# Cross-attention and a quantised feed-forward on one core: all transpositions moved from DMA to TensorE

## The chip, the cores and the metric

The kernel runs on one core of a Trainium2 chip. The core has five engines with instruction streams of their own: TensorE (PE; its weight loads are shown apart as PEld), VectorE (DVE), ScalarE (ACT), GpSimd (POOL) and SyncE (SP), which issues this kernel's DMAs. Each engine takes its work in program order and waits on semaphores for what others make. The metric is the device time of one execution in microseconds (us), lower is better; the time before is 1144.62 us, the median of 3 runs.

## The reference

One block of a transformer on x of shape (8, 1024, 512) with a context of shape (8, 64, 384):

```python
x = x + xattn(layernorm(x), ctx)     # 8 heads of 64, softmax over 64 context rows, then @ Wo + bo
x = x + ffn(layernorm(x))

def ffn(x):                          # inner width 2048
    gate = silu(bitlinear(x, w_gate))
    up = bitlinear(x, w_up)
    return bitlinear(gate * up, w_down)

def bitlinear(x, w):
    s = 127 / max|x| per row         # activations rounded to whole numbers of -128..127
    t = 1 / mean|w|                  # weights rounded to -1, 0, 1
    return (clip(round(x * s)) / s) @ (clip(round(w * t)) / t).T
```

All inputs and outputs are fp32.

## The kernel before

The 8192 rows of x are cut into 64 tiles of 128 rows (`NU` = 64); 8 tiles belong to one batch. The kernel is a single Python function that writes out every engine's order by hand (`manual_schedule`), so the order of the calls is the order on each engine.

**Attention.** For each batch the query and key weights are folded into one matrix `score_w` (`score_products`), and the value and output weights into `value_w` (`value_products`). A tile's scores are x transposed times `score_w`; its attention output is the transposed probabilities times `value_w`. Both are fp32. From tile 8 on, two tiles form a `Pair`, whose product is made of seven quarter products instead of eight (`Seven`); GpSimd forms the sums of blocks that this needs (`add`, and `weight_sums` for the weights). Tiles 0 to 7 are computed alone.

**Feed-forward.** x is normalised, rounded by a magic constant (`round_x` on ScalarE, `shrink_x` on GpSimd) to whole numbers in bf16 (`xq`), and transposed to `xq_t`. `gate_up(s)` makes 512 columns of gate and of up, 8 matmuls with fp8 weights, four times. `gated` applies silu and multiplies. `quantise_h` rounds the product in two halves (ScalarE L614, GpSimd L615) to `hq`, which is transposed to `hq_t`; `output` multiplies it by the down weights in 16 matmuls (L621).

**The pipeline.** A head (the long string `order`) loads the inputs, prepares the first score and value weights, rounds the three feed-forward matrices to -1, 0, 1 in 24 halves, and computes tiles 0 to 6 as far as it can. Each half goes through `round_half`, `shrink_half`, on some paths `clip_half`, and `turn_half`, which transposes it into its place. The loop then runs k from 0 to 64. Iteration k holds the gate and up products of tile k, the rounding of tile k-1's intermediate, the down product of tile k-1, the rounding of x of tile k+1, and attention work for tiles up to k+8: in even iterations a pair's seven score products, in odd ones a pair's seven output products, set between the four calls of `gate_up`. In some batches' iterations the next score and value weights are made too. The last iterations (58 to 63) are arranged apart: rounding comes after the second `gate_up`, and the down products of tiles 61 and 62 stand in iteration 63, after the last tile's rounding (`quantise_h_last`).

**Transpositions.** TensorE needs the left operand transposed. In the head, x of tiles 0 to 7 and the probabilities of tiles 0 to 5 are transposed on TensorE into PSUM (`transpose_x` L353, `transpose_p` L412) and copied out by ScalarE (L357, L416). Everything else is transposed by DMA, issued by SyncE:

- fp32 x and probabilities: GpSimd splits the fp32 words into two 16-bit halves (`split`, L329), one DMA transposes both (L331), and `join` (L338, on ScalarE or GpSimd) puts the words together again;
- `xq` (`turn_x`, L560) and `hq` (L616, and L652 for the last tile), which are bf16;
- the weight halves (`turn_half`, L763), whose fp8 pairs are moved as 16-bit words; this is why the fp8 operands are read with every other byte in the matmuls, and why `as_chunks` and `in_chunks` write even and odd columns apart.

**PSUM.** There are 8 banks. `next_bank` hands them out in turn: banks 0 to 5 for general use, 6 and 7 for projections and products in the head, and in the loop 6 for a pair's running sum "x" and 7 for "y" and "z".

Of the kernel before, what the change touches and what calls it, by code (L numbers as in the profile page):

```python
# [29 lines left out]
def xattn_ffn_kernel(  # L30
# [37 lines left out]


    rounds = {"product": [6, 7], "bank": [0, 1, 2, 3, 4, 5], "x": [6], "z": [7], "y": [7]}  # L70

# [15 lines left out]
    ident = const.tile([P, P], F32, name="ident")  # L87
    make_identity(nc, ident)
    magic = const.tile([P, 1], F32, name="magic")
    nc.vector.memset(magic, MAGIC)  # L90
# [233 lines left out]

    def split(src, name, room):
        halves = apool.tile([P, 2, D], U16, tag=f"{room}2", name=f"split_{name}")
        nc.gpsimd.tensor_copy(halves, src.bitcast(U16).rearrange("p (d h) -> p h d", h=2))  # L329
        halves_t = apool.tile([P, 2 * ND, P], U16, tag=f"{room}2_t", name=f"split_t_{name}")  # L330
        nc.sync.dma_start_transpose(out=halves_t, in_=halves.rearrange("p h d -> p (h d)"))  # L331
        return halves_t

    def join(copy, halves_t, name):
        whole = apool.tile(
            [P, ND, P], F32, tag=f"{name[0]}_t", name=f"{name[0]}_t_{name}", bufs=2
        )
        copy(  # L338
            whole.rearrange("p c t -> p (c t)").bitcast(U16).rearrange("p (m h) -> p h m", h=2),
            halves_t.rearrange("p (h c) t -> p h (c t)", h=2),  # L340
        )
        return whole


    class Attention:
# [13 lines left out]
        def split_x(self):  # L359
            self.x = x_tile(self.i)  # L360
            self.x2_t = split(self.x, f"x_{self.name}", "x")

        def join_x(self):
            self.x_t = join(nc.scalar.copy, self.x2_t, f"x_{self.name}")

        def split_p(self, room="p"):
            self.p2_t = split(self.p.rearrange("p h l -> p (h l)"), f"p_{self.name}", room)

        def join_p(self, copy):
            self.p_t = join(copy, self.p2_t, f"p_{self.name}")  # L370

# [69 lines left out]

    def weight_sums(w, sums):

        w11, w12, w21, w22 = (block(w, i, j) for i in range(2) for j in range(2))
        nc.gpsimd.tensor_tensor(sums[0], w12, w11, ALU.subtract)
        nc.gpsimd.tensor_tensor(w12, w22, w12, ALU.subtract)
        nc.gpsimd.tensor_tensor(sums[1], w22, sums[0], ALU.subtract)
        nc.gpsimd.tensor_tensor(sums[2], w21, sums[1], ALU.subtract)

# [74 lines left out]
    class FeedForward:  # L524
# [30 lines left out]
        def turn_x(self):  # L555
            if self.i >= LATE:
                self.xq_t = late_xq_t[:, ts(self.i % 8, ND), :]
            else:
                self.xq_t = fpool.tile([P, ND, P], BF16, tag="xq_t", name=f"xq_t_{self.name}")
            nc.sync.dma_start_transpose(out=self.xq_t, in_=self.xq)  # L560

# [49 lines left out]
        def quantise_h(self, i):  # L611
            self.hq_t = hq_t_rooms[self.i % 2]
            h, hq = self.h[i], hq_rooms[i]
            nc.scalar.activation(h, h, AF.Identity, bias=magic, scale=self.scale)  # L614
            nc.gpsimd.tensor_scalar(as_chunks(hq), in_chunks(h), -MAGIC, 1.0, ALU.add, ALU.mult)  # L615
            nc.sync.dma_start_transpose(out=self.hq_t[:, ts(i, NF // 2), :], in_=hq)  # L616

# [17 lines left out]
        def quantise_h_last(self):  # L635
# [15 lines left out]
            for i in (1, 0):  # L651
                nc.sync.dma_start_transpose(  # L652
                    out=self.hq_t[:, ts(i, NF // 2), :], in_=hq_rooms[i]
                )
# [59 lines left out]
    def spread_total(i):  # L714
        held["mean", i] = pm = product(f"wtot_ps_{i}")
        nc.tensor.matmul(pm[:, 0:1], lhsT=ones, rhs=held["total", i], start=True, stop=True)
# [24 lines left out]
    def shrink_half(n):  # L741
        tag = ("x2", "p2", "x2_t", "p2_t")[n % 4]
        held["half", n] = wq = apool.tile([P, 2 * D], BF16, tag=tag, name=f"wq_{n}")
        if rounded_by[n] == "a":
            nc.gpsimd.tensor_scalar(wq, part(n), -MAGIC, 1.0, ALU.add, ALU.mult)
        else:
            held["half", n] = signs = wq[:, :D].bitcast(FP8)
            nc.scalar.activation(signs, part(n), AF.Sign, bias=minus_magic, saturate=False)

    def clip_half(n):  # L750
        wq = held["half", n]
        clipped = apool.tile([P, 2 * D], FP8, tag="clipped", name=f"clipped_{n}", bufs=2)
        held["half", n] = clipped
        nc.vector.tensor_scalar(clipped, wq, -1.0, 1.0, ALU.max, ALU.min, saturate=False)

    def turn_half(n):
        i, c, g = n // 8, n % 8 // 2, n % 2
        w_t = weights[i][1]
        if i < 2:
            to = w_t[:, 4 * c + 2 * g :][:, :2].rearrange("p n c f -> p (n c) f")  # L760
        else:
            to = w_t[:, ts(g, 4), ts(c, P)]
        nc.sync.dma_start_transpose(out=to, in_=held["half", n].bitcast(U16))  # L763

# [18 lines left out]
    def ffn_stats(part):  # L783
# [4 lines left out]
        elif part == "b":  # L788
            f.rs = inverse_std(f.mv[:, 1:2], f.name)
        elif part == "c":  # L790
            f.normalise()
            f.scale_x()
        else:
            {"d": f.round_x, "e": f.shrink_x, "f": f.turn_x}[part]()

    def keep(table, i, value):
# [55 lines left out]
        inverse_std.0 copy_v.1.a v.3 sum.0.a v_late.1 copy_v.3.v mean_var.1 copy_v.0.v  # L852
        inverse_std.1 score.3 sum.1.v score.1 score_copies.3.a score_copies.1.a
        score_copies.3.v sum.2.a score_copies.1.v copy_v_late.1.v score.0
        sum.3.a score.2 score_copies.0.v k_late.3 score_copies.2.v score_copies.2.a total.0
# [19 lines left out]
        load_x.3 round.20.g round.22.v turn.15 shrink.16 sums.4 round.18.g transpose_p.3  # L875
        turn.16 shrink.17 residual.2 scores.5 ffn.b copy_p.3 round.19.g turn.17 mean_var.6
        shrink.18 probabilities.4 ffn.c turn.18 shrink.19 attend.3 inverse_std.6 round.23.g
        shrink.20 turn.19 maximum.5 ffn.d turn.20 shrink.21 exp.5 transpose_p.4 residual.3
        ffn.e transpose_x.6 copy_p.4 clip.21 ffn.f copy_x.6 sums.5 attend.4 shrink.22 turn.21
        probabilities.5 shrink.23 turn.22 turn.23 residual.4  # L880
    """
    for entry in order.split():
        kind, n, *on = entry.split(".")
        kinds[kind](int(n) if n.isdigit() else n, *on)
    load_x(4)
    weight_sums(score_w[1], score_sums)


# [17 lines left out]
    pairs = [Pair(i) for i in range(NU // 2)]  # L906
    rounds["product"] = rounds["bank"]
    FIRST = NT // 2
    for k in range(NU + 1):
# [9 lines left out]
        soft = pairs[(k + LEAD - 1) // 2] if not even and FIRST <= (k + LEAD - 1) // 2 < NU // 2 else None  # L919
        joined = pairs[(k + LEAD - 2) // 2] if even and FIRST <= (k + LEAD - 2) // 2 < NU // 2 else None  # L920
        done = pairs[(k + 3) // 2] if not even and 3 <= k < NU - 6 else None
# [3 lines left out]
        if k == 0:  # L925
# [4 lines left out]
            norm_stats(att[LEAD + 1], quant, after)  # L930
        elif (k == 1 or even or k > NU - 6) and k != NU - 6 and quant:
            norm_stats(quant, extra, after)
# [9 lines left out]
        if not last and k != 2 and not (soft and k > NU - 10):  # L942
            round_next(1 if scored or soft else 2)
        if after and even:
            after.split_x()
# [18 lines left out]
        if k == 1:  # L964
            alone.scores(every)
            alone.less_maximum()
            quant.normalise()
# [10 lines left out]
        if soft:  # L978
            soft.tiles[0].sums()
            soft.tiles[0].probabilities()  # L980
            soft.tiles[0].split_p()
        if not even and 1 < k < NU - 6 and (quant or after):
            norm_stats(quant, extra, after)
        early = quant and not soft and k < NU - 6
        if f:
# [15 lines left out]
        if early and k < 2:  # L1001
            quant.quantise_x()
        if k == 1:
            weight_sums(value_w[0], value_sums)
        if soft:
# [27 lines left out]
        if f:  # L1033
            f.gate_up(2)
            f.intermediate(2)
        part("x4")()
        if after and even:
# [6 lines left out]
        if f:  # L1044
            f.gate_up(3)
            f.gated(3)
        if k in (0, 2):
            att[LEAD + k // 2].join_p(nc.gpsimd.tensor_copy)
        if joined and k < NU - 6:
            joined.tiles[1].join_p(nc.gpsimd.tensor_copy)  # L1050
        if quant and not early:
            quant.quantise_x()
        if soft:
            soft.tiles[0].join_p(nc.scalar.copy)
            soft.tiles[1].split_p("px"[k == NU - 7])
            if k == NU - 7:
                soft.tiles[1].join_p(nc.gpsimd.tensor_copy)

# [20 lines left out]
        if k == 1:  # L1079
            alone.sums()  # L1080
            alone.probabilities()
            alone.split_p()
        if after and even:
# [18 lines left out]
        for i in downs(k):  # L1102
            if i == NU - 1:
                ffn[i].output_last()
            else:
                ffn[i].output()


# [29 lines left out]
```

## Time and profile before

| what | value |
|---|---|
| median of 3 runs | 1144.62 us (1144.59 to 1144.74) |
| the profiled execution's own time | 1144.76 us |
| its span, from first to last instruction | 1142.9 us |
| mean granted TensorE clock | 1.000 |
| instructions | 16576 |
| DMA packets, bytes | 320358, 126.93 MB |
| packets under 512 B | 304784 |
| busy share of the 16 DMA engines by queue 1 | 50.8% |

The page gives each engine's busy time, then the chain of work that ended last, followed back from the last instruction. A line of a group reads: line of the source, engine, operation, what is written from what, shape, count, then busy time and mean duration. In a timeline each row is a start, a length, an engine and a line; several instructions in a row are merged and counted with "x". Matmuls overlap, so the distance from one start to the next says what one costs, and its duration doesn't. In a table by windows, each engine has its busy time and in brackets its number of instructions.

### The profile page before, as it was taken

The numbers are of one execution on the slowest core, as the hardware profiler recorded it, in microseconds if no ns is written. First come the engines' busy times: TensorE is split into PE (matmuls) and PEld (weight loads), VectorE is DVE, ScalarE is ACT, GpSimd is POOL, SyncE is SP. The second block draws the span as 40 slices with busy tenths as digits, with TensorE's granted clock in tenths as the row PEclk, the third lists the DMA queues.
The fourth block names the chain that finished last, engine by engine and source line by source line (L and its number), as shares of the span: only waits on it lengthen the run. The fifth ranks groups of instructions, "written<-read, shape, count | busy, mean of one in ns | idle before, by whom it ended". The sixth has DMA issues, their size and how long they took to land.

```text
span 1142.9 us, 16576 instructions
## 1 busy us (share of the span) xinstructions
PE 1132.5 (99%) x5332; PEld 673.7 (59%) x5332; DVE 965.6 (84%) x1908; ACT 725.6 (63%) x935; POOL 743.3 (65%) x850
## 2 busy tenths in 40 slices
PE   8999999999999999999999999999999999999998
PEld 7444566556656666556566666655655665565544
DVE  5887888888888888888898888888888888998885
ACT  3975765766665666666666665676765566666443
POOL 0566776576767757677676867657776676775422
PEclk9999999999999999999999999999999999999999
DMA  9874445455455555354454545545436544453344
GB/s 350 270 158 86 101 87 117 91 106 95 88 114 111 107 102 106 84 93 111 94 114 107 97 100 90 103 106 106 94 79 124 112 101 107 106 102 65 65 96 98
DMA packets 320358, 126.93 MB, mean 111 GB/s; under 512 B 304784, under 2 KB 305552, under 8 KB 319760
## 3 DMA queue, kind: packets, MB, share of 16 engines
q1 hardware_dynamic: 320272, 125.88, 50.8%
q8 instruction: 42, 0.69, 0.2%
q14 instruction: 44, 0.36, 0.1%
HBM read 34.08 MB, written 16.78 MB: 44 GB/s over the span
## 4 chain that ended last, share of the span: by engine, by line
PE 92%; DVE 3%; DMA 2%; POOL 1%; SPq 1%; issue 1%; ACT 0%; DVEq 0%; POOLq 0%; ACTq 0%
PE u_f L574 19%; PE g_f L574 18%; PE down_f L621 18%; PE x_o_pair L482 9%; PE x_s_pair L482 8%; PE z_o_pair L482 4%; PE z_s_pair L482 4%; PE y_o_pair L482 2%; PE y_s_pair L482 2%; PE scores_a L376 2%; PE attn_a L422 2%; DMA score_w<-in_L_ffn_w_gate_dram 2%; PE value_ps L267 1%; PE score_ps L249 1%; PE v_late L205 1%
## 5 line engine op out<-in xcount | busy, mean ns | idle before, releaser
L589 ACT ACTIVATE ln_room<-g_f,dq_x_f 128x512 f32<-128x512 f32 x216 | 148.1, 686 | 210.4 <-PE g_f L574 210.3
L574 PEld LDWEIGHTS <-xq_t_f 128*128 128x128 bf16 x1728 | 169.1, 98 | 186.4 <-issue 2.6
L621 PE MATMUL down_f<-arena,room 128*128 128x512 fp8e4 x1008 | 227.9, 379 | 0.0
L574 PE MATMUL u_f<-arena,xq_t_f 128*128 128x512 fp8e4 x864 | 221.7, 379 | 0.6 <-DVE x_room L428 0.6
L574 PE MATMUL g_f<-wg_t,xq_t_f 128*128 128x512 fp8e4 x864 | 221.7, 379 | 0.0
L615 POOL TENSOR_SCALAR room<-room 128x1024 bf16<-128x1024 f32 x126 | 142.5, 1134 | 104.3 <-ACT room L614 99.1
L590 DVE SCALAR_TENSOR_TENSOR room<-u_f,dq_x_f,ln_room 128x512 f32<-128x512 f32 x216 | 160.9, 745 | 32.0 <-POOL rs_f L298 21.7
L614 ACT ACTIVATE room<-room,magic,scale_h_f 128x1024 f32<-128x1024 f32 x126 | 155.4, 1240 | 22.8 <-DVE scale_h_f L318 22.3
L621 PEld LDWEIGHTS <-room 128*128 128x128 bf16 x1008 | 96.6, 98 | 123.8 <-issue 9.1
L602 DVE TENSOR_REDUCE am_h_f<-room 128x1 f32<-128x1024 f32 x126 | 153.1, 1215 | 2.3
L551 POOL TENSOR_SCALAR xq_f<-ln_room 128x512 bf16<-128x512 f32 x64 | 41.9, 655 | 149.6 <-ACT ln_room L547 146.9
L406 POOL TENSOR_TENSOR p_a<-p_a,rc_a 128x512 f32<-128x512 f32 x64 | 67.1, 1049 | 25.0 <-DVE rc_a L402 14.2
L625 DVE SCALAR_TENSOR_TENSOR x_room<-down_f,dq_h_f,x_room 128x512 f32<-128x512 f32 x63 | 47.1, 747 | 37.7 <-PE down_f L621 37.6
L338 ACT COPY x_t_x_a<-split_t_x_a 128x1024 uint16<-128x1024 uint16 x56 | 75.6, 1350 | 0.0
L391 DVE TENSOR_TENSOR p_a<-p_a,mx_a 128x512 f32<-128x512 f32 x56 | 62.6, 1117 | 1.9
L329 POOL COPY split_x_a<-x_room 128x1024 uint16<-128x1024 uint16 x56 | 63.6, 1137 | 0.0
L329 POOL COPY split_p_a<-p_a 128x1024 uint16<-128x1024 uint16 x58 | 60.1, 1036 | 2.0
L547 ACT ACTIVATE ln_room<-ln_room,magic,scale_x_f 128x512 f32<-128x512 f32 x64 | 51.4, 804 | 8.7 <-DVE scale_x_f L318 8.7
L521 DVE TENSOR_TENSOR x_room<-x_room,x_o_pair 128x256 f32<-128x256 f32 x116 | 48.3, 416 | 8.8 <-PE x_o_pair L482 6.7
L589 ACT ACTIVATE ln_room<-g_f,value_w 128x512 f32<-128x512 f32 x40 | 27.1, 684 | 42.5 <-PE g_f L574 39.4
L574 PEld LDWEIGHTS <-score_w 128*128 128x128 bf16 x320 | 31.3, 98 | 36.1
L286 DVE BATCH_NORM_STATS2 st_a<-x_room 128x6 f32<-128x512 f32 x64 | 42.5, 664 | 6.0 <-DMA x_room<-in_x_dram 6.0
(193 smaller groups left out, 2207.4 us busy)
## 6 DMA issues: line engine op xcount, KB each, us to landing
x_room<-in_x_dram SPq DMA_DIRECT2D x32, 512.0 KB, 4.1
out_dram<-x_room SPq DMA_DIRECT2D x31, 512.0 KB, 2.6
room<-in_L_ffn_w_gate_dram SPq DMA_DIRECT2D x3, 1024.0 KB, 14.4
room<-in_L_ffn_w_down_dram SPq DMA_DIRECT2D x2, 1024.0 KB, 6.3
room<-room SPq DMA_TRANSPOSE x126, 3.2
arena<-in_L_xattn_Wq_dram SPq DMA_DIRECT2D x1, 1024.0 KB, 7.3
score_w<-in_L_ffn_w_gate_dram SPq DMA_DIRECT2D x1, 1024.0 KB, 17.4
wo_sb<-in_L_xattn_Wo_dram SPq DMA_DIRECT2D x1, 1024.0 KB, 15.5
```

The source lines that it names most:

```text
L329: nc.gpsimd.tensor_copy(halves, src.bitcast(U16).rearrange("p (d h) -> p h d", h=2))
L338: copy(whole.rearrange("p c t -> p (c t)").bitcast(U16).rearrange("p (m h) -> p h m", h=2), halves_t.rearrange("p (h c) t -> p h (c t)", h=2),
L391: nc.vector.tensor_tensor(self.p, pm, mx.unsqueeze(2).to_broadcast([P, HEADS, L]), ALU.subtract)
L406: nc.gpsimd.tensor_tensor(self.p, self.p, rc, ALU.mult)
L482: nc.tensor.matmul(pm, lhsT=p[:, c, :], rhs=w[:, c, :], start=first and c == 0, stop=c == 1, skip_group_check=not first,)
L574: nc.tensor.matmul(ps, lhsT=self.xq_t[:, c, :], rhs=rhs.rearrange("p n (f e) -> p n e f", e=2)[:, :, c % 2], start=(c == 0), stop=(c == ND ...
L589: nc.scalar.activation(sg, pg, AF.Silu, scale=self.dq[:, 0:1])
L590: nc.vector.scalar_tensor_tensor(h[:, ts(s % 2, 512)], pu, self.dq[:, 1:2], sg, ALU.mult, ALU.mult)
L602: nc.vector.tensor_reduce(self.am[:, s // 2 : s // 2 + 1], h, AX.X, ALU.max, apply_absolute_value=True)
L614: nc.scalar.activation(h, h, AF.Identity, bias=magic, scale=self.scale)
L615: nc.gpsimd.tensor_scalar(as_chunks(hq), in_chunks(h), -MAGIC, 1.0, ALU.add, ALU.mult)
L621: nc.tensor.matmul(pm, lhsT=self.hq_t[:, f, :], rhs=every_other(wd_t[:, f // 2, :], f % 2), start=(f == 0), stop=(f == NF - 1),)
```

## The change

No DMA transposes any more. Every transposition is a TensorE instruction that writes into PSUM, followed by a copy to SBUF:

- x and probabilities of all tiles use the fp32 transposes of the head, four per tile, and a ScalarE copy; `split` and `join` go.
- `xq` and each half of `hq` go through the new `turn_chunks`: 4 or 8 bf16 transposes into one bank, then one copy (ScalarE for xq and the first half of hq, VectorE for the second half). The calls are put in a list and carried out by `turn_now` at three places of an iteration: after the third `gate_up`, after the fourth, and after the down products. The last tile's two halves are turned where they stand.
- the weight halves are kept in bf16 and transposed in 8 pieces into a bank of their own (bank 5 in the head); VectorE clips them to -1, 0, 1 on the way out of PSUM and writes fp8, even and odd columns in one instruction each.
- bank 5 joins the general banks when the head ends; the loop's products use the general banks from iteration 1 on. Some calls move: two entries of `order`, the four `weight_sums` of the first value weights, and the statistics of iteration 2.

```diff
-    rounds = {"product": [6, 7], "bank": [0, 1, 2, 3, 4, 5], "x": [6], "z": [7], "y": [7]}
+    rounds = {"product": [6, 7], "bank": [0, 1, 2, 3, 4], "weights": [5], "x": [6], "z": [7], "y": [7]}
...
-    def split(src, name, room):
...
-    def join(copy, halves_t, name):
...
+    def turn_chunks(to, chunks, name, copy):
+        n = len(chunks)
+        pt = bank(f"turn_tp_{name}").bitcast(BF16)[:, : n * P].rearrange("p (n m) -> p n m", n=n)
+        for c, chunk in enumerate(chunks):
+            nc.tensor.transpose(pt[:, c, :], chunk, ident_b)
+        copy(to, pt)
+
+    later = []
+
+    def turn_now():
+        for turn in later:
+            turn()
+        later.clear()
...
         def join_x(self):
-            self.x_t = join(nc.scalar.copy, self.x2_t, f"x_{self.name}")
+            self.transpose_x()
+            self.copy_x()
...
-        def join_p(self, copy):
-            self.p_t = join(copy, self.p2_t, f"p_{self.name}")
+        def join_p(self, copy=None):
+            self.transpose_p()
+            self.copy_p()
...
-    def weight_sums(w, sums):
+    def weight_sums(w, sums, which=(1, 3, 2, 4)):
...
-            nc.sync.dma_start_transpose(out=self.xq_t, in_=self.xq)
+            chunks = [self.xq[:, ts(c, P)] for c in range(ND)]
+            to = self.xq_t
+            later.append(lambda: turn_chunks(to, chunks, f"xq_{self.name}", nc.scalar.copy))
...
-            nc.sync.dma_start_transpose(out=self.hq_t[:, ts(i, NF // 2), :], in_=hq)
+            chunks = [hq[:, ts(f, P)] for f in range(NF // 2)]
+            to, copy = self.hq_t[:, ts(i, NF // 2), :], (nc.scalar.copy, nc.vector.tensor_copy)[i]
+            later.append(lambda: turn_chunks(to, chunks, f"hq_{self.name}_{i}", copy))
...
             for i in (1, 0):
-                nc.sync.dma_start_transpose(
-                    out=self.hq_t[:, ts(i, NF // 2), :], in_=hq_rooms[i]
+                turn_chunks(
+                    self.hq_t[:, ts(i, NF // 2), :],
+                    [hq_rooms[i][:, ts(f, P)] for f in range(NF // 2)], f"hq_{self.name}_{i}",
+                    (nc.scalar.copy, nc.vector.tensor_copy)[i],
                 )
...
     def turn_half(n):
...
-        nc.sync.dma_start_transpose(out=to, in_=held["half", n].bitcast(U16))
+        pt = next_bank("weights", f"w_tp_{n}").bitcast(BF16)
...
+            for r in range(2):
+                for k in range(ND // 2):
+                    for e in range(2):
+                        nc.tensor.transpose(pt[:, r, k, e, :], src[:, r, k, e, :], ident_b)
...
+        for e in range(2):
+            nc.vector.tensor_scalar(
+                to[:, :, :, e], pt[:, :, e, :], -1.0, 1.0, ALU.max, ALU.min, saturate=False
+            )
...
     weight_sums(score_w[1], score_sums)
+
+    weight_sums(value_w[0], value_sums, (1, 2))
...
-        if k == 1:
-            weight_sums(value_w[0], value_sums)
+            weight_sums(value_w[0], value_sums, ((4,), (3,))[k])
...
             f.gate_up(2)
             f.intermediate(2)
+        turn_now()
         part("x4")()
...
             f.gate_up(3)
             f.gated(3)
...
+        turn_now()
+        if k == 0:
+            alone.join_p()
...
         if soft:
-            soft.tiles[0].join_p(nc.scalar.copy)
-            soft.tiles[1].split_p("px"[k == NU - 7])
-            if k == NU - 7:
-                soft.tiles[1].join_p(nc.gpsimd.tensor_copy)
+            for t in soft.tiles:
+                t.join_p()
...
         if k == 1:
             alone.sums()
             alone.probabilities()
-            alone.split_p()
+            alone.join_p()
...
                 ffn[i].output()
+        turn_now()
```

## The prediction

> **What bounds the kernel now.** I read the page's busy shares and its chain first, then TensorE's timeline in one steady pair of tiles, then the stages at both ends.
>
> ```profile
> PE 1132.5 (99%) x5332; PEld 673.7 (59%) x5332; DVE 965.6 (84%) x1908; ACT 725.6 (63%) x935; POOL 743.3 (65%) x850
> PE 92%; DVE 3%; DMA 2%; POOL 1%; SPq 1%; issue 1%; ACT 0%; DVEq 0%; POOLq 0%; ACTq 0%
> ```
>
> TensorE is busy for 99% of the span and is 92% of the chain that ended last. A busy PE need not be at its peak, so the timeline of one steady tile has to say it:
>
> ```profile
> 542.13 1.03 PE L482 MATMUL x_s_pair<-arena,x_t_x_a 128*128 128x256 f32 x4
> 542.99 1.03 PE L574 MATMUL g_f<-wg_t,xq_t_f 128*128 128x512 fp8e4 x4
> 543.85 1.03 PE L574 MATMUL u_f<-arena,xq_t_f 128*128 128x512 fp8e4 x4
> 544.72 3.62 PE L621 MATMUL down_f<-arena,room 128*128 128x512 fp8e4 x16
> 548.17 1.03 PE L482 MATMUL y_o_pair<-value_w,p_t_p_a 128*128 128x256 f32 x4
> ```
>
> Read the starts, not the durations. Four matmuls start every 0.86 to 0.87 us and the sixteen of L621 take 3.45 us to the next start: 0.216 us each in every group, without a hole. From 131.77 to 991.5 us TensorE is idle for 0.3 of 859.7 us by the windows, at a granted clock of 1.00. A wait for a transposition by DMA appears nowhere in that stretch on TensorE: the 330 DMA transposes land 2.3 to 4.2 us after issue, hidden. So whatever is given to TensorE lengthens the span by its own time, and what SyncE and GpSimd lose is off the path.
>
> **The removed work.** 330 DMA transposes; GpSimd's 114 splits (63.6 and 60.1 us) and 30 joins (40.0 us); ScalarE's joins of 1.35 and 1.34 us, replaced by copies from PSUM of 0.58 us (L357, L416); six clips (5.6 us) on VectorE. All this is beside TensorE, so I credit nothing, except that ScalarE and GpSimd gain room for what follows.
>
> **The added transposes.** In fp32, 4 for each of the 56 x tiles and 58 p tiles: 456. In bf16, 4 for each of 64 xq tiles, 16 for each of 64 hq tiles, 8 for each of 24 weight halves: 256 + 1024 + 192 = 1472. The trace has fp32 transposes in the head:
>
> ```profile
> 61.03 0.60 PE L412 MATMUL p_tp_a<-ident,p_a 128*128 128x128 f32 x4
> 61.47 0.60 PE L353 MATMUL x_tp_a<-ident,x_room 128*128 128x128 f32 x4
> 61.91 2.10 PE L205 MATMUL k_late<-arena 128*128 128x384 f32 x6
> ```
>
> Four take 0.44 us from start to start, 0.11 us each (their duration is 0.272, but they overlap). That equals a bf16 matmul of 256 columns (32 of L663 in 3.67 us), so fp32 costs two passes over 128 columns: 114 x 0.44 = 50.2 us.
>
> A bf16 transpose isn't in the trace. Above stands the fp32 row, 0.11 us; below stands half of it, 0.055, one pass. What could stop it from reaching the lower end is the weight load that goes with each, 0.098 us in bf16. The nearest rows speak against that limit: the 24 matmuls of "k" (L205, 2.84 us) start every 0.112 us although each load takes 0.192 us, and the 34 of L249 at 19.54 us start every 0.061 us with loads of 0.187. I take 0.060 us: 1280 x 0.060 = 76.8 us in the loop (69.8 to 141). The weights' 192 come with the head.
>
> The Trainium skill, "TensorE: Matmul & The Clock Gate", section "Back-to-back issue gap", gives 81 ns for a sustained stream of load and matmul pairs of 128 columns, more than the isolated gap of about 56 ns; at 81 ns the loop's bf16 transposes would be an estimated 104 us instead of 76.8. The same page's "Part 4: PE-mode transpose" says that one transpose took about 275 ns in a kernel and that the clock gate does not count transposes as activity. The trace has that duration (272 ns) but a spacing of 0.11, and a clock of 1.00 through the head, where they occur; paid at 275 ns, all 1928 would be an estimated 530 us.
>
> **Waits in the loop.** TensorE takes its work in program order, so a transpose whose data is late holds every matmul behind it. For tile k-1's hq and the next xq the place is after the third gate_up of iteration k:
>
> ```profile
> 537.76 1.11 POOL L615 TENSOR_SCALAR room<-room 128x1024 bf16<-128x1024 f32 x1
> 539.54 0.65 POOL L551 TENSOR_SCALAR xq_f<-ln_room 128x512 bf16<-128x512 f32 x1 [0.67 <-ACT ln_room L547]
> ```
>
> The data is done at 538.9 and 540.2 us, TensorE gets there at 542.1: 2 us to spare, in odd iterations about 1 us (523.5 against 524.6), and GpSimd is now free of splits of 1.0 to 1.2 us ahead of it. The regrouped weight sums (L445 to L448, 1.27 us each, as many as before) and the few moved entries of the head's order stay on GpSimd and VectorE beside TensorE: nothing. The evacuations go to ScalarE (half of hq, xq, x, p) and VectorE (half of hq). VectorE's share: 14.5 of 16.9 us per iteration from 400 to 600 us, plus at most 1.2 us (L602, as many elements), while the iteration grows to 18.6; it does not become the bound. The general banks are handed out some 13 to 15 times per iteration instead of 9, so each has to be read out within six hand-outs, some 7 us; the latest reader, L590, starts up to 2.5 us after its product ends. In odd iterations xq is turned after the down product, and its copy then waits on ScalarE with the rounding L614 queued behind it: about 1 us later (0.2 for the transposes, 0.2 to reach ScalarE, 0.6 for the copy), half of that turn's 2 us to spare. I take 0 here; one late copy of 0.7 us in each of 60 iterations would be 42.
>
> **Four places where a wait is sure to appear or to be likely.** First the head, to the first gate_up at 94.57 us:
>
> ```profile
> 32.70:94.57 61.87, 60.59 (x197) 30.29 (x196) 47.96 (x80) 48.86 (x59) 37.38 (x39) 1.00 0.75 189
> ```
>
> Columns after the length: TensorE, loads, VectorE, ScalarE, GpSimd. TensorE gets 192 x 0.060 = 11.5 us. VectorE has 13.9 us idle and gets two clips out of PSUM per half, 48 x 0.75 (L233, 512 elements out of PSUM) less 5.6 = 30.4 us: 16.5 beyond its idle time. All weight halves share one bank, so each turn on TensorE waits for the clips of the one before, and scores, context products and projections queue behind. Bounds: 10.5 (TensorE's part alone at 0.055) and 42 (both in full); I take 20, near VectorE's overflow, since not all its idle time is usable.
>
> Second, iteration 1: lone tile 7 is now turned in place, before the down product.
>
> ```profile
> 113.41 1.03 PE L574 MATMUL u_f<-arena,xq_t_f 128*128 128x512 fp8e4 x4
> 117.31 0.72 ACT L396 ACTIVATE p_a<-p_a,rs_a 128x512 f32<-128x512 f32 x1
> 118.87 0.20 DVE L402 RECIPROCAL rc_a<-sm_a 128x8 f32<-128x8 f32 x1
> ```
>
> TensorE is through with its gate_up at 114.3; the reciprocals end at 119.1 and the multiplication takes 1.05 (L406): 5.8 us of idle TensorE, with the down product behind it. I take 5.5 (3 to 7).
>
> Third, iterations 59 to 62, where rounding starts only after the second gate_up:
>
> ```profile
> 1084.91 1.03 PE L574 MATMUL u_f<-arena,score_w 128*128 128x512 fp8e4 x4
> 1085.28 2.35 POOL L615 TENSOR_SCALAR room<-room 128x1024 bf16<-128x1024 f32 x2 [1.49 <-ACT room L614]
> ```
>
> TensorE reaches the turns at 1085.8, the halves are ready at 1086.4 and 1087.6; with 0.5 us of transposes between, 1.45 us idle, four times: 5.8 (0 to 6).
>
> Fourth, the last tile. Its transposes stand ahead of the two down products that used to cover its rounding:
>
> ```profile
> 1128.94 7.07 PE L621 MATMUL down_f<-arena,room 128*128 128x512 fp8e4 x32
> 1132.14 0.69 DVE L643 TENSOR_SCALAR room<-room 128x1024 bf16<-128x1024 f32 x1
> 1132.31 1.65 POOL L647 TENSOR_SCALAR room<-room 128x512 bf16<-128x512 f32 x2 [7.15 <-ACT room L639]
> ```
>
> TensorE is free at 1128.9, waits to 1132.9 for one half and to 1134.0 for the other, and only then runs 6.9 us of products: 4.6 us idle besides the transposes, less 0.2 for the DMA wait that goes: 4.4 (3.5 to 5).
>
> **Sum.** 50.2 + 76.8 + 20 + 5.5 + 5.8 + 4.4 = 162.7 us. The profiled execution took 1144.76 us (span 1142.9), 0.1 above the median of 1144.62. Forecast: 1307 us.
>
> **Rivals.** (a) The transposes run at one pass and the head hides most of VectorE's share: 50.2 + 69.8 + 10.5 + 3 + 3.5 = 137, or 1282 us. For it: TensorE holds its spacing everywhere. Chance 0.18. (b) A bf16 transpose costs clearly more, from 0.08 us (+26) up to the fp32 row's 0.11 (+64), or a late evacuation holds TensorE in every iteration (+42): 1333 to 1371 us. For it: the load of 0.098 us is longer than one pass, and the banks turn over half again as often. Against it: the rows of L205 and L249. Chance 0.2. (c) Faster: the head is shortened because x loads and chunk loads no longer stand in SyncE's queue behind transposes. Place: the DMA parts of the chain, 2% or 23 us, such as the 3.81 us for x at 90.64. It decides only if 1928 transposes cost less than 23 us together, 0.012 us each, a ninth of the fp32 row: 1122 us at the very best. Chance 0.02. (d) Nothing visible changes, because the DMA transposes are replaced only in places that had slack: against it, every loop product's left operand passes through the changed functions. Chance 0.01.
>
> **Numbers.** The forecast as worked out, 1290 to 1330, has 0.59. The range of 1280 to 1350 takes in (a) and the lower part of (b). Over 0.2% (2.3 us), about what a measurement of this kernel can tell from no change: faster 0.02, within 0.01, slower 0.97.
>
> **What would show it.** Right: no DMA_TRANSPOSE on the page; 7260 matmuls; TensorE still near 97% busy; steady iterations 2.1 us longer (16.4 to about 18.5 without weight products); GpSimd near 580 us; a hole of 4 to 6 us before the down product of iteration 1 and another before the last three; first gate_up near 115 us. Wrong: bf16 groups of eight starting further apart than 0.5 us; regular holes on TensorE released by ScalarE or VectorE copies; a head much longer than 115 us.

## The result and the profile after

The changed kernel takes 1341.95 us (median of 4 runs, 1339.07 to 1343.99) where the kernel before takes 1144.68 in the same session: a ratio of 1.1721, with a 95% interval of 1.1696 to 1.1747. The forecast was 1307 us in a range of 1280 to 1350. The direction and the range held; the forecast was 35 us too low, and the time lies outside the band of 1290 to 1330 that had a chance of 0.59. The execution that was profiled is the 1339.07 us one, with a span of 1337.3 us, 194.4 more than before.

From the page of the changed kernel: first the busy time of each engine, then the shares of the chain that ended last, then three groups of the new operations (busy time, mean ns of one, idle time before them and what ended it).

```profile
PE 1284.4 (96%) x7260; PEld 809.5 (61%) x7260; DVE 1014.3 (76%) x2015; ACT 786.0 (59%) x1093; POOL 585.6 (44%) x706
...
PE 93%; DVE 4%; POOL 2%; issue 1%; ACT 1%; POOLq 0%; DVEq 0%; ACTq 0%
...
L332 ACT COPY room<-turn_tp_hq_f 128x1024 bf16<-128x1024 bf16 x63 | 63.8, 1012 | 35.6 <-PE turn_tp_hq_f L331 35.6
L331 PE MATMUL turn_tp_hq_f<-ident_b,room 128*128 128x128 bf16 x1024 | 69.2, 221 | 8.2 <-POOL room L617 4.4
```

TensorE has 7260 matmuls, 1928 more, and is still the chain, but 96% busy instead of 99: there are now 53 us in which it stands still, where before there were 10. GpSimd fell from 743 to 586 us, and nothing on the chain came of it.

A steady place of the loop, from TensorE's timeline of the changed kernel (start, length, engine, line; the distance from one start to the next is the cost):

```profile
607.32 1.03 PE L576 MATMUL u_f<-arena,xq_t_f 128*128 128x512 fp8e4 x4
608.18 1.06 PE L331 MATMUL turn_tp_hq_f<-ident_b,room 128*128 128x128 bf16 x16
609.08 0.39 PE L331 MATMUL turn_tp_xq_f<-ident_b,xq_f 128*128 128x128 bf16 x4
609.30 1.08 PE L482 MATMUL x_s_pair<-arena,x_t_a 128*128 128x256 f32 x4
```

Sixteen bf16 transposes take 0.90 us and four take 0.22: 0.056 us each, where the forecast had 0.060. The matmul after them starts without a hole. A pair of iterations without weight products went from 32.81 us to 36.96, 2.08 us more for each iteration; the forecast had 2.1.

The excess is in the head. The first gate_up starts at 140.26 us instead of 94.57: 45.7 us later, where the forecast had 20. The windows of the changed kernel, from the first turn of a weight half (the eight transposes that turn it) to the first gate_up (length; then TensorE, loads, VectorE, ScalarE, GpSimd; granted clock; DMA):

```profile
34.40:140.26 105.86, 80.48 (x389) 43.45 (x388) 74.39 (x126) 48.68 (x59) 38.24 (x42) 0.94 0.21 77
```

TensorE is idle for 25 of 106 us, and every other engine for longer: VectorE, which the forecast took for the limit, works for only 74 of them. The clock is 0.94, where the head before had 1.00. No engine is short of time, so it's a matter of who waits for whom. TensorE's timeline and then VectorE's, at the same place of the changed kernel:

```profile
88.80 0.62 PE L771 MATMUL w_tp<-ident_b,wq 128*128 128x128 bf16 x8 [1.39 <-DVE arena L786]
90.90 0.61 PE L771 MATMUL w_tp<-ident_b,wq 128*128 128x128 bf16 x8 [1.48 <-DVE arena L786]
91.34 0.61 PE L410 MATMUL p_tp_a<-ident,p_a 128*128 128x128 f32 x4
92.89 0.62 PE L771 MATMUL w_tp<-ident_b,wq 128*128 128x128 bf16 x8 [0.94 <-DVE arena L786]
```

```profile
87.45 1.29 DVE L786 TENSOR_SCALAR arena<-w_tp 128x512 fp8e4<-128x512 bf16 x2
89.46 1.29 DVE L786 TENSOR_SCALAR arena<-w_tp 128x512 fp8e4<-128x512 bf16 x2 [0.72 <-PE w_tp L771]
91.54 1.29 DVE L786 TENSOR_SCALAR arena<-w_tp 128x512 fp8e4<-128x512 bf16 x2
```

It's a shuttle. Eight transposes fill the one bank, VectorE waits for them, clips it twice (1.29 us), and only then may TensorE fill it again, 1.48 us after it would have. There are 11 such waits, 15.1 us together. While VectorE works TensorE idles, and the other way round. Nor is VectorE behind with its work here: the clips at 89.46 start 0.04 us after the transposes of 88.80 end, and VectorE has idled 0.72 us for them. The other losses of the head are these, again from TensorE's timeline of the changed kernel:

```profile
40.53 1.94 PE L268 MATMUL value_ps<-wo_sb,v_t 64*128 64x512 f32 x2 [4.43 <-DVE v_t L219]
42.40 6.23 PE L374 MATMUL scores_a<-score_w,x_t_a 128*128 128x512 f32 x8
70.05 0.66 PE L350 MATMUL x_tp_a<-ident,x_room 128*128 128x128 f32 x4 [2.68 <-DVE value_w L282]
70.99 5.35 PE L420 MATMUL attn_a<-value_w,p_t_a 128*128 128x512 f32 x8
124.21 0.40 PE L331 MATMUL turn_tp_xq_f<-ident_b,xq_f 128*128 128x128 bf16 x4 [3.21 <-POOL xq_f L551]
124.45 3.65 PE L420 MATMUL attn_a<-value_w,p_t_a 128*128 128x512 f32 x8
```

Three longer waits come to 10.3 us. The first two are for VectorE copies that stand behind clips (in part: 2.05 of the 4.43 us are also there in the first experiment, which has no clips out of PSUM), the third for the xq that is now turned inside TensorE's order. After the first two, eight fp32 matmuls that normally take 3.60 us take 6.23 and 5.35: the granted clock is 0.50 from 40.70 to 47.52 us and from 71.42 to 74.83, and once more from 132.86 to 136.27. At half the rate these 13.6 us cost some 7 us. Sum of the head: 10.7 us of transposes (24 times 0.445), 15.1 and 10.3 of waits less 1.3 of waits that the head before had, 7 of slow clock, 0.2 for the inline xq turn and 0.75 of a later start are 42.8 of 45.7; 3 us are in no row.

### The profile page after: what moved, and what is told of

It is laid out like the page before. It is cut to its first block, busy times and chain, and to the rows that moved or that the text cites. A ratio compares the mean times of both kernels' runs of the same rounds, so it can differ in the third digit from the quotient of the medians.

```text
span 1337.3 us, 19768 instructions
## 1 busy us (share of the span) xinstructions
PE 1284.4 (96%) x7260; PEld 809.5 (61%) x7260; DVE 1014.3 (76%) x2015; ACT 786.0 (59%) x1093; POOL 585.6 (44%) x706
## 4 chain that ended last, share of the span: by engine, by line
PE 93%; DVE 4%; POOL 2%; issue 1%; ACT 1%; POOLq 0%; DVEq 0%; ACTq 0%
PE down_f L625 17%; PE g_f L576 16%; PE u_f L576 16%; PE x_o_pair L482 8%; PE x_s_pair L482 7%; PE turn_tp_hq_f L331 4%; PE z_o_pair L482 4%; PE z_s_pair L482 4%; PE scores_a L374 2%; PE x_tp_a L350 2%; PE p_tp_a L410 2%; PE y_s_pair L482 2%; PE y_o_pair L482 2%; PE attn_a L420 2%; PE value_ps L268 1%; PE turn_tp_xq_f L331 1%
## 5 line engine op out<-in xcount | busy, mean ns | idle before, releaser
L625 PEld LDWEIGHTS <-room 128*128 128x128 bf16 x1008 | 97.2, 98 | 121.8 <-issue 12.1
L551 POOL TENSOR_SCALAR xq_f<-ln_room 128x512 bf16<-128x512 f32 x64 | 44.9, 701 | 262.8 <-ACT ln_room L547 215.7
L404 POOL TENSOR_TENSOR p_a<-p_a,rc_a 128x512 f32<-128x512 f32 x64 | 66.7, 1043 | 58.9 <-DVE rc_a L400 34.3
L332 ACT COPY room<-turn_tp_hq_f 128x1024 bf16<-128x1024 bf16 x63 | 63.8, 1012 | 35.6 <-PE turn_tp_hq_f L331 35.6
L354 ACT COPY x_t_a<-x_tp_a 128x512 f32<-128x512 f32 x64 | 37.4, 585 | 73.2 <-PE x_tp_a L350 70.1
L331 PEld LDWEIGHTS <-room 128*128 128x128 bf16 x1024 | 62.9, 99 | 25.2 <-POOL room L617 7.0
L331 PE MATMUL turn_tp_hq_f<-ident_b,room 128*128 128x128 bf16 x1024 | 69.2, 221 | 8.2 <-POOL room L617 4.4
L332 ACT COPY xq_t_f<-turn_tp_xq_f 128x512 bf16<-128x512 bf16 x54 | 31.8, 588 | 69.8 <-PE turn_tp_xq_f L331 69.8
L297 POOL TENSOR_SCALAR ve_f<-mv_f 128x2 f32<-128x2 f32 (+2 forms) x60 | 11.9, 198 | 110.5 <-DVE mv_f L290 110.1
L521 DVE TENSOR_TENSOR x_room<-x_room,x_o_pair 128x256 f32<-128x256 f32 x116 | 48.3, 416 | 15.1 <-PE x_o_pair L482 14.0
L547 ACT ACTIVATE ln_room<-ln_room,magic,scale_x_f 128x512 f32<-128x512 f32 x64 | 51.9, 811 | 12.6 <-DVE scale_x_f L319 10.2
L531 DVE TENSOR_SCALAR ln_room<-x_room,mv_f,rs_f 128x512 f32<-128x512 f32 x63 | 56.2, 892 | 0.4 <-POOL rs_f L299 0.4
```

Source lines behind the costliest of these rows:

```text
L331: nc.tensor.transpose(pt[:, c, :], chunk, ident_b)
L332: copy(to, pt)
L404: nc.gpsimd.tensor_tensor(self.p, self.p, rc, ALU.mult)
L531: nc.vector.tensor_scalar(self.ln, self.x, self.mv[:, 0:1], self.rs, ALU.subtract, ALU.mult)
L625: nc.tensor.matmul(pm, lhsT=self.hq_t[:, f, :], rhs=every_other(wd_t[:, f // 2, :], f % 2), start=(f == 0), stop=(f == NF - 1),)
```

## Experiments

Three explanations of the head's 26 us above the forecast stood against each other: first, the hand-off through one bank with TensorE's queue behind it; second, VectorE's plain amount of work; third, the other edits of the head (the inline xq turn, the moved entries, one general bank less). For the rest of the time the question was whether the price of each part is what the forecast gave it. Savings are differences of medians to the changed kernel. Its profiled execution is the fastest of its four, 2.9 us below the median and with the highest mean clock, so where rows are added up, profiled executions are compared.

**The weight halves by DMA again**, all else as changed:

```diff
     def turn_half(n):
-        pt = next_bank("weights", f"w_tp_{n}").bitcast(BF16)
...
+        nc.sync.dma_start_transpose(out=to, in_=held["half", n].bitcast(U16))
```

> The changed kernel, but the 24 weight halves go through the old fp8 path and DMA transposes again; all else on TensorE. Theory 1 (the head grew because TensorE's program order now holds turns that wait for one bank and its clips, with all other head work queued behind): the first gate_up returns from 140.3 to about 95 us, the total falls by 44 to 46, to 1296 to 1298 us. Theory 2 (VectorE is overloaded by clips out of PSUM): the same here. Theory 3 (part of the head's growth comes from the moved entries, the later start or the lost bank): the first gate_up stays at 100 us or later and the total above 1303.

Measured: 1300.16 us (1299.63 to 1300.6), ratio 1.1353 [1.1334, 1.1372]: 41.8 us saved. The first gate_up starts at 101.16, so the weights' transposes, with the waits and the slow clock that they bring, cost 39.1 of the head's 45.7 us. The other 6.6 are the third explanation's part, which the forecast had at nothing; the total lies between the two that were expected. The first explanation and the second forecast the same here, so this run can't part them. TensorE's timeline of this run:

```profile
89.71 0.40 PE L331 MATMUL turn_tp_xq_f<-ident_b,xq_f 128*128 128x128 bf16 x4 [2.62 <-POOL xq_f L551]
89.94 5.35 PE L420 MATMUL attn_a<-value_w,p_t_a 128*128 128x512 f32 x8
```

The inline turn waits 2.62 us for its data, and the matmuls behind it run at a slow clock, 1.75 us more; with its own 0.2 that is 4.6 us. The first tile's scores already start 3.5 us later than in the kernel before (38.34 against 34.84), 2.05 of them a wait of `value_ps` for a VectorE copy; which of the other edits brings that wait was not tested. Against these 8.1 us stand 1.3 of waits that the head before had, which leaves about the 6.6.

**The weight turns spread**: the same 24 turns with the same bank and clips, but with half a score or context product set between one turn and the next, and the last four moved into iteration 0.

```diff
-        exp.3 attend.1 turn.9 shrink.11 turn.8 copy_k_late.2.a sums.3 turn.11 sum.8.v sum.11.a
-        probabilities.3 transpose_p.2 turn.10 scores.4 shrink.12 copy_p.2 total.2 residual.1
...
+        exp.3 attend1.1 turn.9 attend2.1 shrink.11 turn.8 copy_k_late.2.a sums.3 sum.8.v sum.11.a
+        probabilities.3 transpose_p.2 scores1.4 turn.11 scores2.4 shrink.12 copy_p.2 total.2 residual.1
+        shrink.13 turn.10 clip.12 transpose_x.5 maximum.4 shrink.14 spread.2 copy_x.5 scale.2 shrink.15
...
```

> The changed kernel, same transposes and clips, same single bank; only the order is other: the head's turns stand between halves of the score and context products (four matmuls each, 1.7 us), and the last four in iteration 0. Theory 1 (a turn waits 1.5 us where it follows another turn, and TensorE's queue behind it): most of the 15.1 us of such waits go and some slow clock, 9 to 16 us less, 1326 to 1333 us. Theory 2 (VectorE has too much work in the head): VectorE's work is the same, at most 3 us less, 1339 or more.

Measured: 1333.07 us (1332.61 to 1334.15), ratio 1.1642 [1.1625, 1.1659]: 8.9 us saved, just at the lower end of what was expected, with the same 2015 instructions on VectorE. The first gate_up starts at 131.40, 8.9 us earlier. Six of the clips, 3.8 us of VectorE's work, now come after it, so a smaller amount of work could explain at most that much of the gain; and VectorE was idle for 31 us of the changed kernel's head. So VectorE's amount of work isn't what held the head. The 11 waits of 15.1 us became seven of 5.8 us, from 0.27 to 1.36 each, two of them for a weight's sum or step instead of a clip. Another wait took part of the gain back:

```profile
116.56 0.61 PE L331 MATMUL turn_tp_xq_f<-ident_b,xq_f 128*128 128x128 bf16 x4 [5.30 <-POOL xq_f L551]
```

TensorE now reaches the xq turn earlier and waits 5.30 us there instead of 3.21. A second bank for the weights, the plainer cure, from which 12 to 20 us less were expected, has no measurement: with only four general banks left, this order of the work deadlocks. What the hand-off would cost with two banks stays open.

**The late turns moved behind ready work**: the turns of the last tile, of iteration 1's lone tile, and of iterations 59 to 62 are put after matmuls whose data is there.

```diff
             for i in (1, 0):
-                turn_chunks(
+                later.append(lambda i=i: turn_chunks(
...
             f.intermediate(2)
-        turn_now()
+        if not last:
+            turn_now()
...
             alone.probabilities()
-            alone.join_p()
+            later.append(alone.join_p)
```

> The changed kernel, with three places mended: the lone tile 7 of iteration 1 is turned after the down product, the last tile's halves after the down products of tiles 61 and 62, and in iterations 58 to 62 the turns stand after the fourth gate_up instead of the third. Theory 1 (the idle spans of TensorE are waits of in-order turns for late data): the hole of 4.3 us with 1.7 of slow clock, the hole of 3.8 with 0.8 and some more of slow clock, and 4 times 1.1 us go: about 15 us less, 1327 us. Rival (the wait only moves: the copies then land late before the down products): at most 5 us less, 1337 or more.

Measured: 1325.82 us (1322.98 to 1327.19), ratio 1.1576 [1.1559, 1.1593]: 16.1 us saved. The end of TensorE's timeline in this run:

```profile
1309.26 7.07 PE L625 MATMUL down_f<-arena,room 128*128 128x512 fp8e4 x32
1316.16 1.06 PE L331 MATMUL turn_tp_hq_f<-ident_b,room 128*128 128x128 bf16 x16
1317.77 3.67 PE L669 MATMUL down_f<-arena,value_w 128*128 128x256 fp8e4 x32 [0.55 <-DVE value_w L332]
```

The two down products that used to cover the last rounding cover it again; what is left is a wait of 0.55 us for a copy. Together the three places cost about what the forecast had reasoned for them (5.5, 5.8 and 4.4: 15.7 us). Between the two profiled executions it is 12.6 us, because the head of this one is 3.1 us longer for another reason (the last section).

**The holes filled with dummy matmuls**: 19 dummy matmuls ahead of iteration 1's turn and 16 ahead of the last tile's. They add work that no one uses and leave the real work as it is.

```diff
             alone.probabilities()
+            fill(19, ident_b, f.xq_t.rearrange("p c t -> p (c t)"))
             alone.join_p()
...
+            fill(16, ident_b, self.xq_t.rearrange("p c t -> p (c t)"))
             for i in (1, 0):
                 turn_chunks(
```

> The changed kernel with dummy matmuls of 512 columns into a spare bank: 19 ahead of tile 7's turn in iteration 1 and 16 ahead of the last tile's turns, some 4.1 and 3.5 us that fit into the holes. If the slow matmuls after a hole come from the clock that is granted after idleness, the down product after iteration 1's hole takes 3.6 us instead of 5.28 and the last tile's 16 transposes 1.06 instead of 1.89; the total falls by 2 to 4 us. If they come from something else (late operands, bank traffic), both lengths stay and the total stays or grows.

Measured, one execution: 1338.02 us, 1.05 us below the fastest run of the changed kernel, whose runs differ by 5 us; one time can't decide it. The answer is in the lines, first of the changed kernel at iteration 1 and at the end, then of this run:

```profile
161.17 1.03 PE L576 MATMUL u_f<-arena,xq_t_f 128*128 128x512 fp8e4 x4
166.53 0.71 PE L410 MATMUL p_tp_a<-ident,p_a 128*128 128x128 f32 x4 [4.33 <-POOL p_a L404]
167.04 5.28 PE L625 MATMUL down_f<-arena,room 128*128 128x512 fp8e4 x16
...
1321.06 1.89 PE L331 MATMUL turn_tp_hq_f<-ident_b,room 128*128 128x128 bf16 x16 [3.80 <-ACT room L643]
1322.74 7.75 PE L625 MATMUL down_f<-arena,room 128*128 128x512 fp8e4 x32
```

```profile
163.68 4.26 PE L337 MATMUL fill<-xq_t_f,ident_b 128*128 128x512 bf16 x18
168.18 0.66 PE L415 MATMUL p_tp_a<-ident,p_a 128*128 128x128 f32 x4 [0.23 <-POOL p_a L409]
168.67 3.62 PE L630 MATMUL down_f<-arena,room 128*128 128x512 fp8e4 x16
...
1322.35 7.07 PE L630 MATMUL down_f<-arena,room 128*128 128x512 fp8e4 x32
```

The same down product takes 5.28 us after a hole of 4.33 us and 3.62 after 4.26 us of dummies; the last ones 7.75 and 7.07. The granted clock is 0.50 from 166.99 to 170.40 us in the changed kernel and 1.00 from 168.30 to 171.71 here. So the slow matmuls come of the idleness before them, not of late operands or banks, and a hole costs more than its own length: 1.65 us more in iteration 1.

**hq by DMA again**: `hq` of all tiles goes by DMA, all else as changed.

```diff
-            later.append(lambda: turn_chunks(to, chunks, f"hq_{self.name}_{i}", copy))
+            nc.sync.dma_start_transpose(out=self.hq_t[:, ts(i, NF // 2), :], in_=hq)
...
-                turn_chunks(
+                nc.sync.dma_start_transpose(
```

> The changed kernel, with hq alone transposed by DMA again (the last tile's too); x, p, xq and weights on TensorE. Theory 1 (a bf16 transpose costs TensorE 0.056 us and no more): 1024 x 0.056 = 57 us, the late waits of 4.4 and the last hole of some 5 go: 65 to 68 us less, 1274 to 1277 us. Rival (evacuations or bank turnover cost beside it): 75 us less or more, 1267 or below. Rival (the holes only move): 57 to 60, 1282 to 1285.

Measured: 1277.45 us (1276.34 to 1279.74), ratio 1.1158 [1.1141, 1.1174]: 64.5 us saved. From one down product to the second next, a pair of iterations with weight products takes 37.44 us here and 39.28 in the changed kernel: 1.84 for 32 transposes, 0.0575 each. From the first gate_up to the end, the two profiled executions differ by 62.7 us. The 1024 transposes at 0.0575 are 58.9 of it, the waits of iterations 59 to 62 are 4.4 and the last tile 5.3; against them stand 6.3 us of a wait that grew, seven times by 0.9. That makes 62.3. TensorE's timeline of this run:

```profile
518.46 0.40 PE L331 MATMUL turn_tp_xq_f<-ident_b,xq_f 128*128 128x128 bf16 x4 [1.59 <-POOL xq_f L551]
```

In the changed kernel that wait is 0.69 us. Take away the 0.9 us of hq turns ahead of it, and it grows by just that: in these iterations GpSimd sets when the turn can start.

**x and probabilities by DMA again** in the loop, with `split` and `join` as before:

```diff
         def join_x(self):
-            self.transpose_x()
-            self.copy_x()
+            self.x_t = join(nc.scalar.copy, self.x2_t, f"x_{self.name}")
...
             alone.probabilities()
-            alone.join_p()
+            alone.split_p()
```

> The changed kernel, with x of tiles 8 to 63 and the probabilities of tiles 6 to 63 split, transposed by DMA and joined again; xq, hq and weights on TensorE. Theory 1 (an fp32 transpose costs 0.11 us): 114 x 0.44 = 50.2 us, and the hole of iteration 1 with its slow clock, 6 us: 54 to 58 less, 1284 to 1288 us. Rival (the splits and joins come back into the way of xq and hq on GpSimd and ScalarE, whose data TensorE now waits for in order): less than 48 saved, 1294 or more.

Measured: 1297.31 us (1297.0 to 1297.91), ratio 1.133 [1.1311, 1.1349]: 44.6 us saved, less than the price of the transposes and iteration 1's hole together (50.2 + 6.0): the total is where the rival put it. The same pair takes 37.53 instead of 39.28 us, 1.75 for four groups: 0.44 each, as forecast. Again the xq waits give part of it back, 1.54 to 1.61 us instead of 0.69 seven times (6.3 us) and 2.16 instead of 0.86 at one more place. The run with hq by DMA waits 1.56 to 1.59 us at the same seven places without a split or a join, so the rival's reason is not needed there: it is enough that TensorE gets to these turns earlier. From the first gate_up on, the profiled executions differ by 45.7 us, where these rows make 48.6; some 3 us are in no row.

**All mended**: the spread turns and the later turns together, still without a DMA transpose; besides, the statement of the head that turns the first xq moves behind the context product of tile 4 (`ffn.f` after `attend2.4`).

> All mended places in one: the turns of the head spread, tile 7 and the last tile turned after down products, the late turns after the fourth gate_up, and the first xq turned after the context product instead of ahead of it (a hole of 3.2 us and its slow clock). If the holes add up independently: 1325.8 of the run with later turns, less the gain of the spread turns (9 to 16), less 3 to 5: 1305 to 1314 us. If they share one cause and the gains overlap: 1318 or more. Still slower than before in any case, by the transposes' own 134 us.

Measured: 1313.45 us (1312.6 to 1313.51), ratio 1.1468 [1.145, 1.1485]: 28.5 us saved, as expected: 8.9 and 16.1, and 3.5 are left for the moved xq turn (3 to 5 expected). The first gate_up starts at 126.26. This is the best all-TensorE version of the study, and it is still 168 us slower than the kernel before.

**The price alone**: the weight halves by DMA and the later turns together.

> The weight halves go by DMA again, as in the first experiment, and at the same time the turns of iteration 1, of iterations 59 to 62 and of the last tile stand behind work that is ready, as in the one with later turns. What is left of the change is the transposes of the loop and few waits. Theory 1 (the costs add up: head of the weights, waits of late turns, and the transposes' own time): 1300.2 less the 16.1 us that later turns saved = 1284 us, 1282 to 1286. Counted from below: 1145 + 50.2 (114 fp32 groups at 0.44) + 71.7 (1280 at 0.056) + 6.6 (rest of the head) + 6.5 (xq waits) = 1280, and up to 6 us more that are in no row yet. Rival (the late turns' waits depended on when the long head let go, or the pieces share waits): the saving is below 10 us, 1290 or more.

Measured: 1285.4 us (1284.04 to 1286.79), ratio 1.1225 [1.1206, 1.1244]. The costs add up: 41.8 and 16.1 us alone, 56.6 together. From the first gate_up (103.27) to the end this run needs 1181.4 us, the kernel before 1048.3: 133.1 more. Transposes are 121.9 of it (114 at 0.44, 1280 at 0.056) and waits in TensorE's timeline 8.6, less 2.3 before; about 5 us are in no row. No version of the study beats the kernel before, and the profile says why none could by these means: even with every hole closed, 121.9 us of transposes lie on an engine that was 99% busy.

## Why the prediction was right, and where it was short

By its own steps, against the profiled execution (194.4 us of span more; forecast 162.7):

| step | forecast, us | in the trace, us |
|---|---|---|
| fp32 transposes | 50.2 | 50.2 (0.44 each group) |
| bf16 transposes of the loop | 76.8 | 71.7 (0.056 each) |
| head | 20 | 45.7 |
| iteration 1 | 5.5 | 6.0 (4.33 and 1.65 of slow clock) |
| iterations 59 to 62 | 5.8 | 4.4 |
| last tile | 4.4 | 5.3 (3.80, and 1.5 of slow clock) |
| waits in the steady loop | 0 | 6.6 |
| in no row | | 4.5 |

The last row probably lies in the steady loop: a pair of iterations grew by 4.15 us, its transposes at these spacings make 4.00, and 0.15 us in each of some 31 pairs would be an estimated 4.6.

**What held.** TensorE bounds the kernel, so each transpose lengthens the span by its own time; the work that left GpSimd and SyncE gave nothing back. The spacing of a bf16 transpose was put at 0.060 us from rows of other matmuls, which start every 0.061 and 0.112 us although their loads take 0.187 and 0.192, and came out within 7%. The Trainium skill, "TensorE: Matmul & The Clock Gate", section "Back-to-back issue gap", gives 81 ns for such a stream of load and matmul pairs and about 56 for the isolated gap; here a sustained run of sixteen pairs is at the lower of the two. No late evacuation holds TensorE in the steady loop, which was rival (b); the time lies in that rival's span, but not by its mechanism. That the range held is therefore partly luck: its upper end was there for that rival, and the head used it up. Rival (a) had the transposes right (one pass each) and the head wrong. The holes of iteration 1 and of the last tile stand at the places named, and moving the turns removed them.

**What failed: the term of the head, 20 us, which measured 45.7.** The step weighed VectorE's work (48 clips of 0.75 us against 13.9 us of idle time) and took the overflow of 16.5 us as the price. The clips are 0.645 to 0.685 us each, and VectorE ended with 31 us idle; the prediction's own sign of being wrong, a head much longer than 115 us, came true. What it should have priced was the loop itself: one bank, eight transposes and two clips that must follow each other, with TensorE's queue behind. The prediction did say that each turn waits for the clips of the one before, and then sized it by a total. The spread order shows that: the same turns and clips, 8.9 us less. The turns came in twos and threes, so nearly half of them met a bank that was still being read, at up to 1.48 us. The step also left out two costs: the slow clock after a hole, and the other edits of the head, 6.6 us where the weights go by DMA again, the inline xq turn above all. Its upper bound of 42 us was near; it was the choice in the middle that was wrong. Two slips beside it move nothing: 1280 transposes at 0.055 are 70.4 us, not 69.8, and an iteration of 16.9 us grows to about 18.9, not 18.6.

**What was missed: 6.6 us of waits for xq.** The prediction read 2 us to spare for xq, but in a pair of iterations without weight sums. Where GpSimd makes the next value weights' sums, it gets to xq late. GpSimd's timeline of the changed kernel, and then TensorE's:

```profile
217.11 1.46 POOL L448 TENSOR_TENSOR arena<-value_w 128x512 f32<-128x512 f32 x1
218.66 1.28 POOL L448 TENSOR_TENSOR value_w<-value_w 128x512 f32<-128x512 f32 x1
219.89 2.62 POOL L448 TENSOR_TENSOR arena<-value_w,arena 128x512 f32<-128x512 f32 x2
222.48 1.08 POOL L551 TENSOR_SCALAR xq_f<-ln_room 128x512 bf16<-128x512 f32 x1
```

```profile
223.62 0.40 PE L331 MATMUL turn_tp_xq_f<-ident_b,xq_f 128*128 128x128 bf16 x4 [0.69 <-POOL xq_f L551]
```

Four sums of 1.3 us stand ahead of L551. It happens once in 8 tiles, seven times, and twice more near the end (0.86 and 0.89). Where less work stands ahead of these turns, TensorE comes earlier and waits longer, which is why undoing the hq or the x and p turns saved less than their price.

## What to carry to other kernels

Work moved onto the engine that bounds the kernel costs its own time, and that part can be read off rows of neighbouring shapes within a few per cent, from start to start. What can't be read off a total is a hand-off: where a bank, a producer and a consumer in strict order follow each other, price one round trip, count how many come without other work between them, and don't compare sums of busy time with idle time. Count a hole of 2 us or more on TensorE dearer than its length, for half the clock may follow it for 3.4 or 6.8 us, and look for slack in the iterations that carry extra work, not in the typical one.

## What the runs showed of the hardware

- A hole on TensorE can halve the clock of what follows: eight matmuls take 6.23 us for 3.60. When this strikes isn't fixed by the hole's length. The same wait of 3.21 us in the head is followed at full speed in the changed kernel (3.65 us, shown above) and at 6.25 us in the run with later turns, whose head has the same order. TensorE's timeline of that run:

```profile
126.23 0.61 PE L331 MATMUL turn_tp_xq_f<-ident_b,xq_f 128*128 128x128 bf16 x4 [3.21 <-POOL xq_f L551]
126.62 6.25 PE L420 MATMUL attn_a<-value_w,p_t_a 128*128 128x512 f32 x8
```

  What decides is how the hole falls on a grid. In these traces the granted clock is 1.00 or 0.50 and changes only at steps of 3.41 us that run through the whole execution: 40.70, 71.42, 132.86 and 166.99 us of the changed kernel lie 9, 18 and 10 steps apart. The windows of two steps and what follows them, in the changed kernel and then in the run with later turns (columns as above):

```profile
119.20:122.62 3.42, 1.49 (x16) 1.28 (x16) 3.35 (x8) 1.20 (x2) 0.86 (x3) 1.00 0.00 0
122.62:126.03 3.41, 1.82 (x8) 1.06 (x9) 1.45 (x4) 1.38 (x3) 2.97 (x4) 1.00 0.01 2
126.03:129.45 3.42, 2.52 (x13) 1.10 (x11) 0.86 (x2) 1.78 (x2) 3.34 (x3) 1.00 0.00 0
```

```profile
121.60:125.01 3.41, 1.42 (x16) 1.17 (x15) 3.34 (x7) 1.21 (x2) 1.23 (x3) 1.00 0.00 0
125.01:131.84 6.83, 5.61 (x10) 2.53 (x11) 1.07 (x3) 3.15 (x4) 6.23 (x7) 0.50 0.00 1
```

  The step ahead has 1.93 us without a matmul in the first and 1.99 in the second. Over the ten traces, every step at full clock with 1.98 us or more of idle TensorE was followed by half the clock (36 steps), and none with up to 1.79; of the six between, the two at 1.83 and 1.88 were and the four at 1.92 to 1.96 were not. By such steps the head ends at 140.26 in one and 143.35 in the other, and the runs of the changed kernel spread over 5 us where the kernel before spreads over 0.2: 1339.07 us at a mean clock of 0.992, 1343.47 and 1343.99 at 0.987. The Trainium skill, the same page, "Part 1: The HAM clock gate", says that a free-running window of about 3.4 us decides; the steps here agree with that. It names a whole idle window as the condition, whereas here some 2 of 3.41 us were enough.
- A VectorE copy of 128 x 1024 bf16 out of PSUM takes 0.678 us and the same on ScalarE 1.012 (L332); the prediction had bounded VectorE's by 1.2.
- Transposes in quantity do not lower the granted clock: it is 1.00 from 177 to 1143 us, with 20 bf16 and some 8 fp32 transposes in each iteration.
